# Loading the first layer's input transposed, with the row statistics spread through memory, in a two-layer graph kernel

## The chip, the cores and the metric

One core of one Trainium2 chip. The metric is device microseconds of one execution, as the median of several; lower is better. Profiles are of one execution each.

## The reference, cut to what matters

128 independent graphs ("entries") of 128 nodes with 512 features, all in fp32. Layer 0 is a pre-normalised attention with 8 heads, layer 1 a graph attention. The part that the change touches is the first line of layer 0: the normalisation over the features, followed by a relu and by projections.

```python
h = jnp.maximum(_layernorm(x, axis=-1), 0.0)           # x: (128, 128, 512)
x = x + _L0_gnn_ref(h, adj, adj, Wq, bq, Wk, bk, Wv, bv, Wo, bo, 128)
h = jnp.maximum(_layernorm(x, axis=-1), 0.0)
x = x + _L1_gnn_ref(h, adj, L1_gnn_W, L1_gnn_a)
```

A layer norm needs the mean and the reciprocal deviation of each row (node). The projections contract over the features, so TensorE wants `h` with features on the partitions.

## The kernel before

It loads an entry with nodes on the partitions, where the statistics of a row are one number per partition, normalises there, and turns the result with four TensorE transposes; ScalarE's relu takes it out of PSUM.

```python
def norm0(b):                       # VectorE
    mv, rstd = st0.pop(b)
    nc.vector.tensor_scalar(hns[b], xs[b], mv[:, 0:1], rstd, op0=OP.subtract, op1=OP.mult)

def hidden_T(b):                    # TensorE, ScalarE
    pt = ps1.tile([P, C, P], F32, name="pt", tag="ps1")
    for c in range(C):
        nc.tensor.transpose(pt[:, c, :], hn[:, c * P : (c + 1) * P], ident)
    nc.scalar.activation(hTs[g][:, :, i, :], pt, AF.Relu)
```

The program is one loop of ticks, one entry a tick, in a fixed order on each engine. Entries are projected in groups of four: in the ticks of one group the projections `pp` of the next are made, so tick 0 already needs all of entries 4 to 7. Ahead of the loop come the transposes and projections of the first group and the constants (a matmul for `c`, eight VectorE products with their transposes `pu` for `u`).

```python
for b in range(G):                  # G = 4
    stats0(b); norm0(b); hidden_T(b)
for n in range(2 * C):
    evict = qk_unit(0, n)           # projection of group 0
    stats0(G + n // 2) if n % 2 == 0 else norm0(G + n // 2)
    evict()
    if n % 2: hidden_T(G + n // 2)
...
constants()
for t in range(B + 3):              # scores(t), qk_unit(g + 1, ...), values(t), ..., output1(t - 2)
```

## Time and profile before

| | before |
|---|---|
| time, median of 3 | 2844.6 us |
| span of the profiled run | 2843.2 us |
| TensorE / VectorE / ScalarE busy | 99% / 52% / 41% |
| first scores (tick 0), tick 1, tick 2 | 57.6 / 74.3 / 92.8 us |
| a tick of the steady loop | 21.80 us |

The prediction below shows the lines that carry this. Three transfers of before are these (what is moved, the queue that issues it, how often, its size, and the median time from issue to landing); the estimates for the new transfers were taken from them:

```profile
x<-in_x SPq DMA_DIRECT2D x128, 256.0 KB, 2.9
out<-x SPq DMA_DIRECT2D x128, 256.0 KB, 2.0
adj<-in_adj SPq DMA_DIRECT2D x128, 64.0 KB, 2.5
```

These move pieces of 512 bytes to 2 KB.

### The profile page before, as it was taken

To read this page: it belongs to the slowest core of one execution; us is meant where nothing else is said; L and a number is where in the kernel's file an instruction comes from. 1 tells how busy PE (TensorE), PEld (TensorE's weight loads), DVE (VectorE), ACT (ScalarE), POOL (GpSimd) and SP (SyncE) were. 2 spreads that over 40 slices of the span, in tenths; PEclk is the share of its full clock that TensorE was granted. 3 is DMA by queue.
4 is the path that set the end of the run, shared out by engine and by line. 5 is a ranking of instruction groups with operands and counts; after the bars stand their busy time and mean duration, and the time that the engine had idled before them with its cause. 6 is when DMAs were issued, how large, how long until landed. Compare 5 with 4: busy or idle time off the path is not lost.

```text
span 2843.2 us, 33011 instructions
## 1 busy us (share of the span) xinstructions
PE 2808.9 (99%) x11920; PEld 1481.9 (52%) x11920; DVE 1477.1 (52%) x2961; ACT 1174.7 (41%) x3460; POOL 396.4 (14%) x647
## 2 busy tenths in 40 slices
PE   7999999999999999999999999999999999999997
PEld 3555555555555555555555555555555555555554
DVE  3455555555555554555455545554555555555545
ACT  2444444444444444444444444444444444444343
POOL 1111111111111111111111111111111111111101
PEclk9999999999999999999999999999999999999999
DMA  4000010001001100100010001000100010011000
GB/s 143 19 29 28 29 37 28 28 29 38 28 29 32 34 28 28 36 30 29 28 37 29 28 28 38 28 29 28 38 28 28 28 37 29 28 32 31 17 23 19
DMA packets 78546, 92.05 MB, mean 32 GB/s; under 512 B 9904, under 2 KB 42672, under 8 KB 78384
## 3 DMA queue, kind: packets, MB, share of 16 engines
q1 hardware_dynamic: 76800, 89.95, 9.8%
q8 instruction: 94, 1.54, 0.2%
q14 instruction: 68, 0.56, 0.1%
q10 hardware_dynamic: 1584, 0.01, 0.0%
HBM read 56.37 MB, written 33.55 MB: 32 GB/s over the span
## 4 chain that ended last, share of the span: by engine, by line
PE 98%; DVE 1%; ACT 1%; issue 0%; DMA 0%; POOL 0%; DVEq 0%; ACTq 0%
PE pm L124 46%; PE pp L162 32%; PE sc L185 5%; PE pc L216 5%; PE pg L267 4%; PE pa L205 4%; PE pt L145 2%; PE pb L245 0%; ACT at L192 0%; DVE at L187 0%; DVE nmx L189 0%; DVE at L199 0%; DVE junk L294 0%; DMA x<-in_x 0%; PE pm L285 0%
## 5 line engine op out<-in xcount | busy, mean ns | idle before, releaser
L192 ACT ACTIVATE at<-at,nmx 128x128 f32<-128x128 f32 x1024 | 395.9, 388 | 380.7 <-DVE nmx L189 380.7
L277 DVE SCALAR_TENSOR_TENSOR x<-pm,x 128x512 f32<-128x512 f32 x128 | 88.5, 691 | 798.1 <-ACT ez L276 798.1
L162 PE MATMUL pp<-hT,wq 128*128 128x512 f32 x1024 | 476.2, 608 | 0.7 <-ACT hT L146 0.7
L124 PE MATMUL pm<-w,gT 128*128 128x512 f32 x1024 | 462.9, 595 | 1.5 <-ACT gT L269 1.5
L117 POOL TENSOR_SCALAR rstd<-mv 128x1 f32<-128x1 f32 x256 | 134.8, 526 | 2343.9 <-DVE mv L114 2343.9
L124 PE MATMUL pm<-wo,cxT 128*128 128x512 f32 x1024 | 460.7, 593 | 0.5 <-ACT cxT L221 0.5
L124 PE MATMUL pm<-wv,hT 128*128 128x512 f32 x1024 | 460.6, 593 | 0.0
L162 PE MATMUL pp<-hT,wk 128*128 128x512 f32 x1024 | 460.6, 593 | 0.0
L124 PEld LDWEIGHTS pm<-wo,cxT 128*128 128x128 f32 x1024 | 185.0, 191 | 220.3 <-issue 219.6
L162 PEld LDWEIGHTS pp<-hT,wq 128*128 128x128 f32 x1024 | 185.2, 191 | 201.5 <-issue 185.5
L124 PEld LDWEIGHTS pm<-wv,hT 128*128 128x128 f32 x1024 | 185.3, 190 | 187.4 <-issue 187.4
L124 PEld LDWEIGHTS pm<-w,gT 128*128 128x128 f32 x1024 | 185.3, 191 | 186.8 <-issue 184.5
L162 PEld LDWEIGHTS pp<-hT,wk 128*128 128x128 f32 x1024 | 185.3, 191 | 186.4 <-issue 186.4
L248 DVE TENSOR_TENSOR w<-w,neg 128x128 f32<-128x128 f32 x128 | 37.4, 292 | 441.7 <-ACT w L247 441.7
L167 ACT ACTIVATE kT<-pp,bk 128x512 f32<-128x512 f32 x128 | 88.1, 688 | 357.9 <-PE pp L162 357.9
L174 ACT COPY v<-pm 128x512 f32<-128x512 f32 x128 | 75.0, 586 | 359.9 <-PE pm L124 359.8
L276 ACT ACTIVATE ez<-pm 128x512 f32<-128x512 f32 x128 | 76.4, 597 | 315.9 <-PE pm L124 315.9
L118 POOL TENSOR_TENSOR rstd<-rstd,mhalf 128x1 f32<-128x1 f32 x256 | 199.3, 778 | 21.4
L192 ACT ACTIVATION_READ_ACCUMULATOR at<-at,nmx 128x1 f32 x1024 | 191.4, 187 | 0.0
L112 DVE BATCH_NORM_STATS2 st<-x 128x6 f32<-128x512 f32 x256 | 177.0, 691 | 8.8 <-DMA x<-in_x 4.2
L267 PEld LDWEIGHTS pg<-w,h 128*128 128x128 f32 x1024 | 134.9, 193 | 72.6 <-issue 68.3
L187 DVE TENSOR_TENSOR at<-sc,adj 128x1024 f32<-128x1024 f32 x128 | 156.7, 1224 | 17.9 <-PE sc L185 15.1
(57 smaller groups left out, 2856.9 us busy)
## 6 DMA issues: line engine op xcount, KB each, us to landing
x<-in_x SPq DMA_DIRECT2D x128, 256.0 KB, 2.9
out<-x SPq DMA_DIRECT2D x128, 256.0 KB, 2.0
adj<-in_adj SPq DMA_DIRECT2D x128, 64.0 KB, 2.5
adjT<-in_adjT SPq DMA_DIRECT2D x128, 64.0 KB, 2.5
wq<-in_wqT SPq DMA_DIRECT2D x1, 1024.0 KB, 7.2
wk<-in_wkT SPq DMA_DIRECT2D x1, 1024.0 KB, 8.0
wv<-in_wvT SPq DMA_DIRECT2D x1, 1024.0 KB, 10.0
wo<-in_woT SPq DMA_DIRECT2D x1, 1024.0 KB, 12.1
```

The costliest lines, as they stand in the source:

```text
L112: nc.vector.bn_stats(st, src)
L117: nc.gpsimd.tensor_scalar_add(rstd, mv[:, 1:2], EPS)
L118: nc.gpsimd.tensor_tensor(rstd, rstd, mhalf, OP.pow)
L124: nc.tensor.matmul(pm, lhsT[:, c, :], w[:, c, :], start=(c == 0), stop=(c == C - 1))
L162: nc.tensor.matmul(pp, w[:, c, f * P : (f + 1) * P], hTs[g][:, c].rearrange("p b s -> p (b s)"), start=(c == 0), stop=(c == C - 1),)
L185: nc.tensor.matmul(sc[:, s * C + i, :], qT[r, i, cols], kT[r, i, cols], start=True, stop=True)
L187: nc.vector.tensor_tensor(at, sc, adjs[b][:, None, :].to_broadcast([P, H, S]), OP.mult)
L192: nc.scalar.activation(at[:, j, :], at[:, j, :], AF.Exp, bias=nmx[:, j : j + 1], accum_out=sums[:, j : j + 1])
L205: nc.tensor.transpose(pa[:, j, :], at[:, j, :], ident)
L216: nc.tensor.matmul(pc[s * D : (s + 1) * D, i, :], vs[b][:, head * D : (head + 1) * D], ats[b][:, s * C + i, :], start=True, stop=True,)
L267: nc.tensor.matmul(pg[:, c, :], h2[:, c * P : (c + 1) * P], w, start=True, stop=True)
L277: nc.vector.scalar_tensor_tensor(xs[b], pw, 0.0, xs[b], op0=OP.max, op1=OP.add)
```

## The change

The aim is to take the transposes off TensorE. The host gives a second, transposed copy of the input. For entries from 4 on, the plain copy is loaded only for the statistics; these (two numbers a row) are stored to memory, 4 bytes at a time, so that they lie in a line, and fetched back spread over all partitions; VectorE then normalises in the transposed layout with two instructions. Entries 0 to 3 keep the old way. Besides, the first four statistics are made together, and the constants move from the front of the loop into ticks 0 and 1.

```diff
+    def spread0(b):
+        mv, _ = st0.pop(b)
+        rows0[b] = dram.tile([2, P], F32, name="rows0")
+        nc.sync.dma_start(rows0[b].rearrange("s p -> p s"), mv)
+    def fetch0(b):
+        r = rows0[b]
+        rows0[b] = small.tile([P, 2, S], F32, name="mr", bufs=3)
+        nc.sync.dma_start(rows0[b].rearrange("p s k -> p (s k)"), r.rearrange("s p -> (s p)").partition_broadcast(P))
+    def hidden(b):
+        nc.vector.tensor_tensor(h, h, mr[:, 0:1, :].to_broadcast([P, C, S]), OP.subtract)
+        nc.vector.scalar_tensor_tensor(h, h, 0.0, mr[:, 1:2, :].to_broadcast([P, C, S]), op0=OP.max, op1=OP.mult)
 ...
         for b in range(G):
             stats0(b)
+        for b in range(G):
             norm0(b)
             hidden_T(b)
+            load_x0(G + b)
         for n in range(2 * C):
+            b = G + n // 2
             evict = qk_unit(0, n)
-            stats0(G + n // 2) if n % 2 == 0 else norm0(G + n // 2)
+            if n % 2 == 0:
+                stats0(b)
+                spread0(b)
+                fetch0(b)
+            else:
+                load_x0(b + G)
             evict()
-            if n % 2:
-                hidden_T(G + n // 2)
+            if n > 2 and n % 2:
+                hidden(b - 1)
+        hidden(2 * G - 1)
 ...
-        constants()
         for t in range(B + 3):
+            if ahead < B:
+                fetch0(ahead)            # stored one tick earlier
+            if ahead + 1 < B:
+                spread0(ahead + 1)
 ...
+            if t == 1:
+                spread_u()
-            if ahead < B:
-                hidden_T(ahead)
+            if ahead < B:
+                hidden(ahead)
+                if t == 0:
+                    constant_c()
+                    constant_u()
```

(Statistics now kept in place in `mv`.)

## The prediction

> **What bounds the kernel now.** I read the page's busy shares and chain first, then the timeline of TensorE in order of time, then VectorE's groups by form, then the first 75 us of every engine and of the DMA queue.
>
> ```profile
> PE 2808.9 (99%) x11920; PEld 1481.9 (52%) x11920; DVE 1477.1 (52%) x2961; ACT 1174.7 (41%) x3460; POOL 396.4 (14%) x647
> PE 98%; DVE 1%; ACT 1%; issue 0%; DMA 0%; POOL 0%; DVEq 0%; ACTq 0%
> PE pm L124 46%; PE pp L162 32%; PE sc L185 5%; PE pc L216 5%; PE pg L267 4%; PE pa L205 4%; PE pt L145 2%; PE pb L245 0%; ACT at L192 0%; DVE at L187 0%; DVE nmx L189 0%; DVE at L199 0%; DVE junk L294 0%; DMA x<-in_x 0%; PE pm L285 0%
> ```
>
> TensorE is 99% busy and is 98% of the chain that ended last, so only TensorE time counts, and only what is taken out of it or out of its idle stretches. A busy share alone could hide slack, so I looked at two neighbouring ticks of the loop (one tick is one batch entry): the last one with transposes `pt` and the first without.
>
> ```profile
> 2643.41 1.16 PE L185 MATMUL sc<-kT,qT 64*128 64x128 f32 x16
> 2644.50 3.70 PE L162 MATMUL pp<-hT,wq 128*128 128x512 f32 x8
> 2648.04 0.27 PE L245 MATMUL pb<-ident,ws 128*128 128x128 f32 x1
> 2648.15 3.60 PE L124 MATMUL pm<-wo,cxT 128*128 128x512 f32 x8
> 2651.58 0.60 PE L145 MATMUL pt<-ident,hn 128*128 128x128 f32 x4
> 2652.02 3.60 PE L124 MATMUL pm<-wv,hT 128*128 128x512 f32 x8
> ...
> 2665.21 1.16 PE L185 MATMUL sc<-kT,qT 64*128 64x128 f32 x16
> ...
> 2669.95 3.60 PE L124 MATMUL pm<-wo,cxT 128*128 128x512 f32 x8
> 2673.38 3.60 PE L124 MATMUL pm<-wv,hT 128*128 128x512 f32 x8
> ...
> 2686.57 1.16 PE L185 MATMUL sc<-kT,qT 64*128 64x128 f32 x16
> ```
>
> The columns are start, length, engine, line and operation. The tick with `pt` lasts 2665.21 - 2643.41 = 21.80 us, the one without 2686.57 - 2665.21 = 21.36. No line shows idle time. The kernel before thus already contains, four times (ticks 120 to 123), the tick that the change would make everywhere: 0.44 us shorter, the 0.44 between 2651.58 and 2652.02.
>
> Third, the start, where TensorE does stand idle:
>
> ```profile
> 46.67 0.60 PE L145 MATMUL pt<-ident,hn 128*128 128x128 f32 x4
> 47.10 3.60 PE L285 MATMUL pm<-wo,bv 128*128 128x512 f32 x8
> 52.19 0.29 PE L300 MATMUL pu<-ident,ucol 128*128 128x128 f32 x1 [1.48 <-DVE junk L294]
> ...
> 57.63 2.08 PE L185 MATMUL sc<-kT,qT 64*128 64x128 f32 x16
> 59.65 4.33 PE L162 MATMUL pp<-hT,wq 128*128 128x512 f32 x8
> ```
>
> The constants take TensorE from 47.10 to 57.63: 3.4 us of matmul, then 7.1 us at the pace of VectorE's eight products. Afterwards matmuls run slow for a moment (2.08 for 1.16 and 4.33 for 3.70). The page's median times from issue to landing are 2.0 us for `out` and 2.5 for `adj`.
>
> **What the Trainium skill says.** "TensorE: Matmul & The Clock Gate", section on the PE-mode transpose, gives about 275 ns for a transpose in a kernel. The trace has a median of 273 ns, but that is latency: four cost 0.44 us of TensorE's time, so 0.11 each, and that I use. The same page, section on the HAM clock gate, says that an idle window of about 3.4 us takes the clock to half; the slow matmuls after the constants agree. "VectorE: DVE Perf Modes", section on the TRN2 errata, has (N+151)/0.96 ns for an fp32 tensor_tensor, 691 for N = 512; the trace has 684 to 691 for most two-input forms and 660 for the shift. "DMA: Bandwidth & Descriptors", section on two DMAs through one engine, says they are not ordered, so the fetch of the statistics must wait for the completion of their store. No trace here yet shows a store of 4-byte elements.
>
> **The change part by part.**
>
> *Transposes removed.* Batch entries 4 to 127 lose `pt` and its ScalarE relu. In the loop that is ticks 0 to 119; from tick 2 on, 118 x 0.44 = 51.9 us off TensorE. The four of entries 4 to 7 save 1.7 more ahead of the loop.
>
> *VectorE work.* norm0 (542 ns) goes, hidden's subtraction (about 660 to 690) and its scalar_tensor_tensor (691) come: +0.83 us per tick. They land in VectorE's block that ends with the shift:
>
> ```profile
> 999.91 0.54 DVE L135 TENSOR_SCALAR hn<-x,mv,rstd 128x512 f32<-128x512 f32 x1
> ...
> 1001.19 0.66 DVE L151 TENSOR_TENSOR x<-x,c 128x512 f32<-128x512 f32 x1
> 1008.18 0.69 DVE L277 SCALAR_TENSOR_TENSOR x<-pm,x 128x512 f32<-128x512 f32 x1 [6.34 <-ACT ez L276]
> ```
>
> The block ends at 1001.85, and VectorE then waits 6.34 us for `ez`. The addition fits there with over 5 us to spare: cost on the path 0.
>
> *Memory.* Per tick one 128x1 KB fetch, a 1 KB scattered store and one 256 KB load more. In the steady loop store and fetch lie a tick apart, about 21 us, against 2 to 3 us each. The transposed input is issued behind the previous output, about 11 us before VectorE wants it. DMA is at a mean of 32 GB/s. Cost 0.
>
> *PSUM.* Without `pt` a tick uses eight of the four-deep tiles, not nine; the values' matmul takes the buffer of `pp`, evicted only 0.4 us earlier by ScalarE. Ticks 120 to 123 have that rotation and show no wait.
>
> *The start.* Here the new round trip is on the path. Entry 4's rows now load behind all weights. In the kernel before, the load in the same place of the same queue (the ninth x) was issued at 20.71 and took 5.4 us, landing at 26.1. Then: statistics 0.9, GpSimd 1.0, store (my estimate from the 2.0 of `out`: 2.5), fetch (from the 2.5 of `adj`: 2.6), and 1.3 for the two hidden instructions. The order of issue chains them: store 4 at 28.1, fetch 4 lands 33.3, and VectorE, held by hidden(4), only then makes the statistics of entry 6. Store 6 goes at 36.5 and fetch 6 lands at 41.8; behind hidden(5) come the statistics of 7, store 7 at 40.2 to 42.7, fetch 7 to 45.4, hidden(7) done at 46.8. The second group's projection, in tick 0, needs all of entries 4 to 7.
> TensorE would be ready earlier: the statistics of the first four now run together, so the first projection starts near 12.6 where it was 15.62; eight units of 3.44, plus 2.3 for the slow first one, end near 42.4, the first scores near 43.9. So about 2.9 us idle, and the projection starts at 46.8, where it was 59.65.
>
> *The constants.* From 46.8: projection 4.3 (slow clock), values and second projection 6.9, `pa` 0.9, the constant's matmul 3.4 (ends 62.3), `pc` 1.0: tick 1's scores at 63.3. VectorE finishes the addition to c at 63.1, the eight products (0.73 each) at 69.0 and the shift at 69.6. TensorE meanwhile has scores and projection to 67.9 and waits for the last product until about 69.2, 1.4 us. The later harm: the scores of tick 1 are masked 5 us late, ScalarE's exponentials end at 75.3, then two copies of `pu` and the eviction of `pp` at 77.1. The output projection is done at 72.7, and the values' matmul needs `pp`'s buffer, because the two `pu` tiles use up the rotation: 4.4 us idle, and some 1.5 of slow clock behind it. Values, projection, `pa`, the known wait of 1.1 for its copy, and `pc` give tick 2's scores at about 88.5. They were at 92.81.
>
> *The sum.* Before tick 2: -4.3. Ticks 2 to 119: -51.9. Ticks 120 to the end, 178.0 us, unchanged. Total -56.2: 2844.6 - 56.2 = 2788.4, so 2788 us, 2.0% less. The move of the constants itself is worth next to nothing.
>
> **The rivals.**
> 1. *The start hides better.* If store and fetch are 2.0 us each, the chain to hidden(7), with four stores and a fetch in a row, is about 2.6 us shorter, and the idle time nearly goes. If also ScalarE frees `pp` in time, tick 1 loses only 1.5 and the time is about 2779. For: `out` lands in 2.0. Against: that median is for 2 KB pieces; the 4-byte bias loads took 3.7 to 5.3 among other traffic.
> 2. *The round trip is longer.* At 4 us a store, the chain adds 6 us: 2794. For: the 4-byte pieces.
> 3. *VectorE or a transfer becomes a bound in the loop.* VectorE goes from 52% to about 56%, and a late transfer blocks it in order, so `ez`'s reader and the PSUM release behind it would slip. A wait of 0.1 us a tick costs 12 us (2800); one of the full 0.44 gives all back (2840). Against: the slack above, and the clean ticks 120 to 123.
> 4. *Transposes were hidden anyway.* Excluded by 21.80 against 21.36.
>
> **Range and chances.** The steady gain of 52 is nearly certain; the start is uncertain by some 5 us either way, with a small tail upward from rival 3. Range 2782 to 2797. A gain of 2% is 2787.7, practically my number, so it is close to a coin toss; the tail upward tips it: faster 0.44, same 0.54, slower 0.02.
>
> **What would show it right or wrong.** Right: ticks of 21.36 all through, scores following each other with no idle on TensorE; VectorE's wait for `ez` shorter by about 0.8 us a tick; the second group's first projection near 47 us, preceded by an idle stretch that ends with hidden of entry 7; an idle stretch of about 4 us ahead of tick 1's values, ended by ScalarE's eviction of `pp`; tick 2's scores near 88. Wrong: ticks over 21.4, TensorE idle in the loop ended by VectorE's hidden or by the eviction of `pp`, VectorE idle until a DMA of the statistics or of the transposed input, or a scattered store well over 3 us.

## The result, and the profile after

The changed kernel took 2825.76 us (median of 4, 2823.47 to 2826.31) against 2845.43 for the kernel before. The ratio is 0.9929, with a 95% interval of 0.9912 to 0.9947: faster, but by 0.7% and not by 2.0% (so "same" where 2% is asked for), and outside the range.

The page of the changed kernel, busy shares and chain:

```profile
PE 2750.6 (97%) x11424; PEld 1431.5 (51%) x11424; DVE 1581.7 (56%) x3085; ACT 1100.9 (39%) x3336; POOL 415.2 (15%) x647
...
PE 94%; DMA 3%; DVE 1%; ACT 1%; SPq 0%; issue 0%; POOL 0%; ACTq 0%; DVEq 0%
```

TensorE's work fell by 58 us (2808.9 to 2750.6). But the chain, which had no share of DMA, has 3% of it, and TensorE is no longer 99% busy. So the question is where. First the steady loop, TensorE in order of time (start, length, instruction):

```profile
998.45 1.16 PE L225 MATMUL sc<-kT,qT 64*128 64x128 f32 x16
...
1003.18 3.60 PE L142 MATMUL pm<-wo,cxT 128*128 128x512 f32 x8
1006.62 3.60 PE L142 MATMUL pm<-wv,hT 128*128 128x512 f32 x8
...
1019.81 1.16 PE L225 MATMUL sc<-kT,qT 64*128 64x128 f32 x16
```

1019.81 - 998.45 = 21.36 us, with no idle time, and every tick from 2 to 119 has that length. The transposes are gone and nothing took their place. VectorE's block is longer and its wait for `ez` shorter, 5.02 us where it was 6.34:

```profile
1012.45 0.69 DVE L184 SCALAR_TENSOR_TENSOR hT<-hT,mr 128x512 f32<-128x512 f32 x1
...
1019.58 0.69 DVE L317 SCALAR_TENSOR_TENSOR x<-pm,x 128x512 f32<-128x512 f32 x1 [5.02 <-ACT ez L316]
```

Then the start of the program:

```profile
40.51 1.34 PE L225 MATMUL sc<-kT,qT 64*128 64x128 f32 x16
81.12 5.20 PE L202 MATMUL pp<-hT,wq 128*128 128x512 f32 x8 [39.28 <-DVE hT L184]
```

TensorE stands idle for 39.28 us ahead of the second group's first projection, waiting for the last `hidden`. The gain of the steady loop is paid back here, in one piece. By the starts of the same work in the three columns:

| us from the start | before | predicted | after |
|---|---|---|---|
| first projection | 15.6 | 12.6 | 12.8 |
| TensorE ready for the second group's projection | - | 43.9 | 41.8 |
| second group's projection starts | 59.7 | 46.8 | 81.1 |
| scores of tick 2 | 92.8 | 88.5 | 122.7 |
| a tick, 2 to 119 | 21.80 | 21.36 | 21.36 |
| end of the span | 2843.2 | about 2787 | 2821.7 |

(The 41.8 is the 81.12 less the wait of 39.28. The predicted 2787 is the 2788 less the 1.4 us by which the time before exceeded its span.)

What held `hidden`? The chain of waits in order of time, the pieces of it that are transfers and the two instructions at its end (start, length, what):

```profile
28.77 8.38 DMA rows<-mv
...
38.06 10.65 DMA rows<-mv
...
49.63 11.41 DMA rows<-mv
...
61.96 12.28 DMA rows<-mv
...
74.25 5.38 DMA mr<-rows
...
79.65 0.70 DVE hT L183
...
80.38 0.69 DVE hT L184
```

`rows<-mv` is the store of an entry's statistics: 1 KB that takes 8 to 12 us. Four of them stand in a row, 42.7 us together, because the sync queue issues the fetch of an entry only when its store has landed, and the next store behind that fetch. In the steady loop a store takes about as long, and there it costs nothing, since its fetch comes a tick later:

```profile
mr<-rows SPq DMA_DIRECT2D x124, 128.0 KB, 3.6
...
rows<-mv SPq DMA_DIRECT2D x124, 1.0 KB, 9.3
```

### The profile page after: what moved, and what is told of

The parts are those of the page before. It is cut to its first block, busy times and chain, and to the rows that moved or that the text cites. A ratio compares the mean times of both kernels' runs of the same rounds, so it can differ in the third digit from the quotient of the medians. Undisturbed runs are those within 1.5% of the kernel's fastest.

```text
span 2821.7 us, 33182 instructions
## 1 busy us (share of the span) xinstructions
PE 2750.6 (97%) x11424; PEld 1431.5 (51%) x11424; DVE 1581.7 (56%) x3085; ACT 1100.9 (39%) x3336; POOL 415.2 (15%) x647
## 4 chain that ended last, share of the span: by engine, by line
PE 94%; DMA 3%; DVE 1%; ACT 1%; SPq 0%; issue 0%; POOL 0%; ACTq 0%; DVEq 0%
PE pm L142 46%; PE pp L202 31%; PE sc L225 5%; PE pc L256 5%; PE pg L307 4%; PE pa L245 4%; DMA rows<-mv 2%; ACT at L232 1%; PE pb L285 0%; DMA mr<-rows 0%; DMA c<-in_bo 0%; DVE nmx L229 0%; DVE at L227 0%; DVE junk L337 0%; DMA x<-in_x 0%; SPq L79 0%
## 5 line engine op out<-in xcount | busy, mean ns | idle before, releaser
L135 POOL TENSOR_SCALAR mv<-mv 128x1 f32<-128x1 f32 x256 | 135.8, 530 | 2303.4 <-DVE mv L132 2303.2
L317 DVE SCALAR_TENSOR_TENSOR x<-pm,x 128x512 f32<-128x512 f32 x128 | 88.5, 691 | 641.9 <-ACT ez L316 641.9
L142 PEld LDWEIGHTS pm<-wv,hT 128*128 128x128 f32 x1024 | 194.5, 190 | 248.2 <-issue 244.4
L288 DVE TENSOR_TENSOR w<-w,neg 128x128 f32<-128x128 f32 x128 | 37.4, 292 | 441.5 <-ACT w L287 441.5
L136 POOL TENSOR_TENSOR mv<-mv,mhalf 128x1 f32<-128x1 f32 x256 | 200.0, 781 | 21.4
```

The lines of the kernel that those rows point to most:

```text
L135: nc.gpsimd.tensor_scalar_add(rstd, rstd, EPS)
L136: nc.gpsimd.tensor_tensor(rstd, rstd, mhalf, OP.pow)
L142: nc.tensor.matmul(pm, lhsT[:, c, :], w[:, c, :], start=(c == 0), stop=(c == C - 1))
L317: nc.vector.scalar_tensor_tensor(xs[b], pw, 0.0, xs[b], op0=OP.max, op1=OP.add)
```

## The experiments

The theory after the result: the loss is only the serial round trip at the start, and it is that long because stores of 4-byte pieces are slow. Rivals: late loads or the moved constants make the loss; or the store is slow for another reason than its pieces (a fixed latency, its number of pieces, waiting behind other transfers). Eleven kernels were run. Those with three rounds or more have an interval; the others are one look. In the diffs lines are shortened or joined with `;`, and left-out lines are marked ` ...`.

### 1. The old start for entries 4 to 7

```diff
-            if n % 2 == 0:
-                stats0(b); spread0(b); fetch0(b)
-            else:
-                load_x0(b + G)
+            if n % 2 == 0:
+                stats0(b)
+            else:
+                norm0(b); load_x0(b + G)
             evict()
-            if n > 2 and n % 2:
-                hidden(b - 1)
+            if n % 2:
+                hidden_T(b)
```

(and the plain copies of entries 4 to 7 are loaded where the transposed ones were, with eight buffers instead of four.)

> Entries 4 to 7 are normalised and transposed on the engines as before; only entries from 8 on take their statistics through memory. Theory A (the whole loss is the serial round trip at the start): no idle stretch of 39 us, units end near 42.1 us, tick 1's scores near 59, tick 2's near 83, ticks of 21.36 after that: 2784 us (2782 to 2787). Rival B (the loss is in the start but of another kind, such as loads that come late or the constants in ticks 0 and 1): an idle stretch of over 10 us remains in ticks 0 or 1 and the time stays above 2800.

Measured: 2783.1 us, ratio 0.978 (0.9765 to 0.9795), faster than the kernel before by 2.2%, with a correct result. TensorE at the point where it had idled for 39 us:

```profile
42.23 1.16 PE L225 MATMUL sc<-kT,qT 64*128 64x128 f32 x16
43.33 3.70 PE L202 MATMUL pp<-hT,wq 128*128 128x512 f32 x8
```

No wait. Tick 2's scores come at 81.5 us and the ticks after it last 21.36. Theory A holds: the round trip at the start is the whole loss, and the constants, still in ticks 0 and 1, are not. (The run also loads the plain copies of entries 4 to 7 earlier. That late loads are not the loss is shown by experiments 10 and 11, which keep them late and wait 3.09 and 1.69 us.)

### 2. All four stores ahead of the fetches

```diff
+            if n == 0:
+                for j in range(G, 2 * G):
+                    stats0(j); spread0(j)
+                for j in range(G, 2 * G):
+                    fetch0(j)
```

(with a fourth buffer for the fetched rows)

> All four statistics of entries 4 to 7 are stored before any is fetched. Theory A1 (a store's 8 to 12 us is latency, and the loss is that four of them stand in a row): the stores overlap, the last lands near 40 to 42 us, the fetches near 47, the second group's projection starts near 48 instead of 81: about 2792 us. Rival A2 (the memory takes scattered 4-byte pieces one by one, so stores queue behind each other at 7 to 8 us each): the last store lands near 59, the projection starts near 66: about 2811 us.

Measured: 2800.7 us, ratio 0.9842 (0.9828 to 0.9857), between the two expectations. TensorE's wait falls from 39.28 us to 15.22. The transfers of that stretch, 28 to 52 us:

```profile
mr<-rows SPq DMA_DIRECT2D x4, 128.0 KB, 9.7
rows<-mv SPq DMA_DIRECT2D x4, 1.0 KB, 12.6
```

In single landings: the first two stores, issued at 28.8 and 29.6, landed at 37.4 and 38.1, the other two, issued at 30.5 and 31.3, at 47.7 and 47.9. So they overlap two by two, and neither "pure latency" nor "strictly one after the other" is right. And something new shows: the first two fetches were issued at 37.4 and 38.1, when their own stores had landed, and landed only at 51.6 and 51.9, after the later stores. A slow store seems to hold up transfers that need nothing from it.

### 3. Pieces of 8 bytes

```diff
-        rows0[b] = dram.tile([2, P], F32, name="rows0")
-            nc.sync.dma_start(rows0[b].rearrange("s p -> p s"), mv)
+        rows0[b] = dram.tile([P, 2], F32, name="rows0")
+            nc.sync.dma_start(rows0[b], mv)
```

(`hidden` then reads the fetched row with a step of two, which cost VectorE nothing: 683 and 692 ns an instruction, as without the step.)

> The statistics of an entry are stored as 128 pieces of 8 bytes in the order in which they lie, and sorted by strides when VectorE reads them, instead of 256 pieces of 4 bytes; bytes and places are otherwise the same. If a store's time goes with the number of pieces[...], it is near 4.8 us, four of them save about 15 us or more: 2806 to 2812 us. If it is a fixed latency of small writes, it stays at 8 us and the time at 2826.

Measured: 2800.2 us, ratio 0.9842 (0.9825 to 0.9858). The store lands after 4.9 us in the steady loop instead of 9.3, and after 3.5 to 5.4 us at the start. So it is not a fixed latency. The four stores of the start took 18.2 us together instead of 42.7, and the fetches 3.8 to 4.8 each; that saves more than the 14 to 20 us expected, because the stores of the changed kernel were not 8.4 us each but up to 12.3. Half the pieces, but also half as many pieces in the same stretch of memory: the next run parts the two.

### 4. Stores of other layouts, one in each of ticks 122 to 129

```diff
+            if 122 <= t < 130:
+                probe(t - 122)    # nc.scalar.dma_start(<unused memory in layout t - 122>, c_sb[...])
```

> The changed kernel with one further store to unused memory in each of ticks 122 to 129, from a constant tile, on ScalarE's queue, each of another layout; time within 3 us of 2826. What they tell: 256 x 4 bytes packed (pa) should take 7 to 9 us as in the kernel. If the cost is per piece wherever it goes, 256 x 4 bytes each 64 bytes (pc64) or 512 bytes (pd512) apart take as long, 128 x 8 (pb) and 128 x 4 (ph) half, 32 x 4 (pg16) about 2.5 us. If it is pieces that share a line of memory, pd512 falls to 2 to 3 us and pa does not. 128 x 64 bytes (pe64) tells whether larger packed pieces suffer too; 128 x 512 bytes (pf512) should take about 2 us like the output.

Measured: 2823.2 us (one run, state unknown), and these eight issues (name, queue, size, us to landing):

```profile
pf<-c ACTq DMA_DIRECT2D x1, 64.0 KB, 1.5
pa<-c ACTq DMA_DIRECT2D x1, 1.0 KB, 8.1
pb<-c ACTq DMA_DIRECT2D x1, 1.0 KB, 3.3
pc<-c ACTq DMA_DIRECT2D x1, 1.0 KB, 1.6
pd<-c ACTq DMA_DIRECT2D x1, 1.0 KB, 1.6
pe<-c ACTq DMA_DIRECT2D x1, 8.0 KB, 2.0
pg<-c ACTq DMA_DIRECT2D x1, 0.1 KB, 3.0
ph<-c ACTq DMA_DIRECT2D x1, 0.5 KB, 6.8
```

256 pieces of 4 bytes packed (`pa`) take 8.1 us in a stretch where few other transfers run. The same 256 pieces laid 64 bytes apart (`pc`) or 512 apart (`pd`) take 1.6 us, as little as 64 KB in pieces of 512 bytes (`pf`, 1.5). So neither the number of pieces nor their size makes the store slow by itself; it takes dense packing. 128 pieces of 4 bytes packed (`ph`) take 6.8 us and 128 of 8 bytes packed (`pb`) 3.3: the same number, half as many in each 64 bytes, less time. Among packed pieces of 4 bytes the number does count (3.0, 6.8 and 8.1 us for 32, 128 and 256). The expectation that `ph` and `pb` would be alike was wrong. `pg`, 32 packed pieces, took 3.0 where 2.5 was expected. Each of these is one observation.

### 5. The constants alone, in the kernel before

```diff
-        constants()
         for t in range(B + 3):
+            if t == 1:
+                spread_u()
 ...
                 attn_T(t)
+                if t == 0:
+                    constant_c()
+                    constant_u()
```

> The kernel before with the constants alone moved as in the change (the constant of the shift and VectorE's products in tick 0, their spreading in tick 1); nothing else. As the prediction had it, the move is worth next to nothing: 2843 to 2846 us. The run with the old start for entries 4 to 7 says otherwise: there ticks 0 and 1 took 39.3 us with the constants in them, where before the constants in front and those two ticks took 45.7, of which 0.9 were transposes: so about 5.5 us less: 2840 us.

Measured: 2841.1 us against 2846.1, ratio 0.9983 (0.997 to 0.9995). The move is worth about 5 us. It costs one wait in tick 1, the same 2.92 us as in the changed kernel and in the run with the old start, where the values' matmul waits for ScalarE's copies of `pu`:

```profile
71.41 3.70 PE L142 MATMUL pm<-wv,hT 128*128 128x512 f32 x8 [2.92 <-ACT u_src L347]
```

(This line is from the run with the old start.)

### 6. Fetches that wait for no store

Wrong result: entries 4 to 7 fetch 256 numbers of the input instead of their statistics. The stores are still made.

```diff
+        if b < 2 * G:
+            nc.sync.dma_start(<rows0[b]>, x[b][0, 0 : 2 * P].partition_broadcast(P))
+            return
```

> Wrong result on purpose: for entries 4 to 7 the fetch reads 256 numbers of the input, which no one stores, so it waits for no store; the stores are still made, on the same queue. If the loss is only the wait for a store's completion before its fetch is issued, the fetches land 3 to 5 us after their issue (from 33 us on), the second group's projection starts near 45 us, and the time is near 2789. If a load that is queued behind such a store is held until the store has landed, the fetches land near 38, 42 and later, the projection starts between 50 and 65 us, and the time is 2795 to 2809.

Measured: 2807.0 us (one run, state unknown). The second group's projection starts at 63.3 us, with a wait of 21.35:

```profile
63.34 5.70 PE L206 MATMUL pp<-hT,wq 128*128 128x512 f32 x8 [21.35 <-DVE hT L188]
```

The fetches need no store and yet take 10.7 us (window 28 to 62 us):

```profile
mr<-in_x SPq DMA_DIRECT2D x4, 128.0 KB, 10.7
...
rows<-mv SPq DMA_DIRECT2D x4, 1.0 KB, 11.0
```

So removing the wait on the semaphore does not free the fetch: issued at 29.4, right behind the first store, it landed at 38.7, just after that store's 38.6.

### 7. The constants early

The run with the old start, and the constants ahead of the loop again, but VectorE's products issued while TensorE projects the first group.

```diff
+        constant_u()        # behind the loop over n
         load_x(0)
 ...
         stats0(2 * G + 1)
+        spread_u()
+        constant_c()
         for t in range(B + 3):
-            if t == 1: spread_u()
 ...
-                if t == 0: constant_c(); constant_u()
```

> A candidate to beat both: entries 4 to 7 as before, the statistics through memory only from entry 8 on, and the constants ahead of the loop but their products on VectorE while TensorE projects the first group. If the idle 2.9 us in tick 1 come only from the two spread tiles and ScalarE's copies there, they vanish: first scores near 46.6, tick 2's near 79.2 us, 2780.8 us against 2783.1 with the constants in ticks 0 and 1. If the products hold up VectorE or their tiles hold up the first tick, it is 2783 or more.

Measured: 2780.2 us, ratio 0.9773 (0.9758 to 0.9788), correct. Tick 2's scores come at 79.5 us, and the wait of 2.92 us is gone. It is the best version, 65.9 us under the kernel before in the medians of that comparison, where the change as made saved 19.7. Its lead over experiment 1, 2.9 us in the medians, is not clear of noise by the intervals, which overlap; the trace shows what was gained.

### 8. The same fetches, the stores on another queue

As experiment 6 (wrong result), with the four stores issued by GpSimd.

```diff
-            nc.sync.dma_start(rows0[b].rearrange("s p -> p s"), mv)
+            (nc.gpsimd if b < 2 * G else nc.sync).dma_start(rows0[b].rearrange("s p -> p s"), mv)
```

> As the run whose fetches of entries 4 to 7 read what no one stores (wrong result on purpose), but those four stores are issued by GpSimd on its own queue. If a queue is held up behind a slow store, the fetches on the other queue are now free: they land within 3 to 5 us of their issue, the projection of the second group starts near 44 us and the time is near 2788, whatever the stores take. If the hold is in the memory or in the DMA engines that all queues share, the fetches come as late as in the other run.

Measured: 2789.2 us (one run, state unknown), and no long wait on TensorE. The time is that of the first expectation, but the transfers say the second. Three fetches were issued before the first store or with it (25.7, 27.9 and 28.9 us; the store at 29.0) and landed after 3.5, 3.5 and 4.1 us. The fourth was issued at 31.7, on a queue that no longer carried any of these stores, and took 9.4:

```profile
mr<-in_x SPq DMA_DIRECT2D x1, 128.0 KB, 9.4
```

The time fell because the sync queue, rid of the stores, no longer waits for statistics and issues three of four fetches ahead of the first store. So the hold is in what the queues share, as far as one fetch in one run shows it. The Trainium skill ("DMA: Bandwidth & Descriptors", on issuing engines not being separate DMA queues) says that transfers of all issuers run on the same 16 engines and interleave; this run agrees, and suggests that the hold of a slow store is shared in the same way.

### 9. Only the order of the first statistics

```diff
         for b in range(G):
             stats0(b)
+        for b in range(G):
             norm0(b)
             hidden_T(b)
```

(in the kernel before, with a fourth buffer for `hn`)

> The kernel before with only the order of the first four entries changed: four statistics, then four normalisations (a fourth buffer for hn with it). By the trace of the changed kernel the first projection starts at 12.8 us instead of 15.6 and is not slowed by the clock (3.5 us instead of 5.7), 4.9 us in all: 2840.5 us. The prediction gave it 3 us and kept the slow first projection; if that held, 2842.5 us.

Measured: 2841.1 us against 2846.1, ratio 0.9984 (0.9971 to 0.9996), so 5.0 us in the medians; but in the profiled run, 2842.0, only 3. There the first projection does start at 12.9 us, and is slow:

```profile
12.90 5.70 PE L162 MATMUL pp<-hT,wq 128*128 128x512 f32 x8 [0.69 <-ACT hT L146]
```

This is the prediction's slow first projection. In the changed kernel's profile the same work took 3.70 us. The runs with equal work up to there fall into both kinds (3.70 in experiments 1 to 3, 5.59 and 6.02 in 8 and 11). So about 2 us of the start differ from run to run. That it depends on when the clock comes up was not tested.

### 10. The unread stores 64 bytes apart

Experiment 6 again (wrong result, stores on the sync queue), with one difference: each number of those four stores goes 64 bytes from the next.

```diff
-        rows0[b] = dram.tile([2, P], F32, name="rows0")
+        rows0[b] = dram.tile([2, P, 16], F32, name="rowsw")     # entries 4 to 7
+        dst = rows0[b][:, :, 0]
```

> As the run whose fetches of entries 4 to 7 read what no one stores (wrong result on purpose, 2807 us), stores on the same queue again, but each number of those four stores is written 64 bytes from the next instead of 4. As many pieces, as many bytes. If packing within 64 bytes makes the stores slow, they land in 2 to 3 us, the loads behind them in 3 to 5, the idle stretch before the second group's projection shrinks from 21 us to below 5, and the time is 2785 to 2791. If it is the number of pieces or the path from a chip memory to the outer one, the run repeats the 2807.

Measured: 2788.5 us (one run, state unknown). The wait on TensorE is 3.09 us instead of 21.35. That wait:

```profile
44.85 5.40 PE L208 MATMUL pp<-hT,wq 128*128 128x512 f32 x8 [3.09 <-DVE hT L190]
```

In the window 28 to 62 us:

```profile
mr<-in_x SPq DMA_DIRECT2D x4, 128.0 KB, 4.1
...
rowsw<-mv SPq DMA_DIRECT2D x4, 1.0 KB, 2.7
```

Equal pieces, equal bytes, equal order of issue: 11.0 us become 2.7 for the stores, 10.7 become 4.1 for the fetches behind them. The packing is the cause, in the kernel as in the probe. A fetch from such a layout would itself be in pieces of 4 bytes, so this is a test and not a cure.

### 11. Both cures in the change's own start

Pieces of 8 bytes (experiment 3) and the four stores ahead of the fetches (experiment 2), correct result.

> The changed kernel's own start, correct result, with both cures: 128 pieces of 8 bytes a store, and all four stores ahead of the fetches. Stores of 3 to 4 us each that queue behind each other from 29 us on: last landing 37 to 42, fetches 41 to 46, projection of the second group 44 to 50 against 81 in the changed kernel: 2786 to 2794 us; either cure alone gave 2800. If the two cures save the same time and not each its own, about 2798.

Measured: 2787.5 us, ratio 0.9797 (0.9781 to 0.9814), which straddles 2%. The second group's projection starts at 45.8 us with a wait of 1.69:

```profile
45.78 3.70 PE L202 MATMUL pp<-hT,wq 128*128 128x512 f32 x8 [1.69 <-DVE hT L184]
```

The two cures together bring the changed kernel to the time that was predicted for it without them.

## Why the prediction was wrong

**What bounds the kernel, and the gain of the steady loop: right.** 118 ticks of 21.36 us were predicted and found. VectorE's additional work and the further transfers of the loop cost nothing, and rivals 3 and 4 are out. VectorE's wait for `ez` shortened by 1.3 us a tick where about 0.8 was expected, because the tick shortened too.

**The start: the step that failed.** The words are "store (my estimate from the 2.0 of `out`: 2.5), fetch (from the 2.5 of `adj`: 2.6)". The mechanism was right: the order of issue chains the stores, and the second group's projection waits for hidden(7). The cost of a link was too small: a store was put at 2.5 us and took 8.38, 10.65, 11.41 and 12.28, together 42.7; the last fetch was put at 2.6 and took 5.4. From the first store's issue to the end of hidden(7) the prediction had 18.7 us, the trace 52.3, so 33.6 more. The projection came 34.3 us late (81.1 for 46.8), and tick 2's scores 34.2, of the 34.7 by which the end of the profiled span missed. That is nearly the whole miss. (The profiled run, 2823.5, was the fastest of the four.)

The path shifted with the cost. By the times of the prediction's own start only three stores were on it (4, 6 and 7), with the fetch of 4, hidden(4) and the statistics of 6 between the first two, and store 5 ran beside these; its rivals count "four stores and a fetch in a row" instead, which does not agree with that. In the trace it was four stores and a fetch, and VectorE was no link: it had finished the statistics of entry 6 at 44.6 us, and their store was issued only at 49.6, when store 5 had landed.

The estimate went wrong because it took the time of a transfer of other pieces, 2 KB each, and allowed only half a microsecond for the 4-byte pieces. The prediction even said that no trace showed such a store, and among its signs of being wrong is "a scattered store well over 3 us", which is what came. Rival 2 named the right direction, but stopped at 4 us a store, and the range with it. The prediction also did not have the second effect, that what is issued behind such a store is held too: experiments 6 and 10 show it in the fetches, 10.7 us against 4.1.

**The constants: wrong by about 5 us where nothing stalls.** "The move of the constants itself is worth next to nothing" rested on an idle time of 4.4 us in tick 1, 1.4 us for the products and 1.5 of slow clock behind. In experiment 1 the idle time was 2.92 and there was neither a wait for the products nor a slow matmul. Experiment 5 measures the gain. In the changed kernel itself this part of the sum came out, by luck: from the second group's projection to tick 2's scores it took 41.5 us (81.12 to 122.65) where 41.7 were predicted. The idle time there was 2.92 too, and no slow matmul followed it; but the eight transposes `pu` with their wait for the products took 2.92 us (1.11 in experiment 1), and the projection behind the stall was slower than predicted (5.20 us; the granted clock was still 0.50 from 82 to 84 us). The slow matmul behind the idle time did come in experiments 2, 6 and 10, with 5.29 to 5.40 us for 3.70.

**The first projection** was put at 12.6 and came at 12.8. The 2.3 us for a slow first projection were not there in the changed kernel's profile; other runs have them.

**The slow clock.** The prediction took the slow matmuls after the constants as agreeing with the idle window that it cites. In the trace of before the granted clock is indeed 0.50 there (56 to 60 us), but TensorE's single waits ahead of it were 1.48 us at most, among short transposes, so that trace alone does not show an idle window at work. In the changed kernel the clock does fall within a long idle stretch, the one from 41.8 us on: 0.79 on the mean from 42 to 50 us, 0.50 from 50 to 84.

What stays open: why exactly packed pieces are slow (the times of `pa`, `ph`, `pb` and `pg` follow no single count that was tried), why the stores of the start grew from 8.4 to 12.3 us, and why the fetches of the start took 4.9 to 5.4 us where the steady loop has 3.6.

## What to carry to other kernels

A transfer that is new in kind, here by the size and the packing of its pieces, can't be sized from the transfers that the trace has; where the whole gain hangs on it, ask how long it may take before it hurts, and set the range by that. A latency that a pipelined loop hides is paid in full ahead of the loop, once per link of the chain there: let the first iterations go another way, or issue all first links before the second ones. A row of numbers that is turned through memory should not be stored in 4-byte pieces side by side where something waits for it.

## What the Trainium skill lacked or had wrong

- "DMA: Bandwidth & Descriptors", section Specifications, gives 512 B as the least size for full rate and says that smaller transfers are read, changed and written back. Size alone did not make a store slow here: 256 pieces of 4 bytes landed after 1.6 us when 64 or 512 bytes apart, and after 8.1 us when packed; 64 KB in 512-byte pieces took 1.5. The page says nothing of small pieces that lie side by side.
- The same page does not say that a slow store to memory holds up transfers issued after it, on its queue or another (it says so of stalled writes, but for transfers between cores, in the section on back-pressure in remote DMA). Here a fetch of 128 KB took 3.5 us ahead of such stores, 9.3 behind one on its own queue, and 9.4 behind one on another.
- "TensorE: Matmul & The Clock Gate", section on the PE-mode transpose, has the latency of a transpose (about 275 ns; 273 here), but not what it takes of TensorE's time in a stream: four cost 0.44 us, 0.11 each.
